# A fused adaLN block on one core: ring and order of the modulation rows, and the first three convolution blocks

## The chip, the core and the metric

The kernel runs on one core of a Trainium2 chip. The metric is the device time of one execution in microseconds; lower is better. A core has a matmul engine (TensorE, PE in the profile, with its weight loads as PEld), VectorE (DVE), ScalarE (ACT), GpSimd (POOL) and SyncE (SP, which here only issues transfers), and 16 DMA engines that carry every transfer. TensorE writes to PSUM, from which VectorE and ScalarE read.

## What is computed

The input u has shape (4, 1024, 2048). A small product makes six modulation vectors of 2048 for each of the four batch entries; then come a state-space convolution and a dense layer with a low-rank update, each behind a layer norm and a gate. Cut to what matters:

```python
mod = (silu(c) @ wmod).reshape(4, 6, 1, -1)        # wmod: 2048 x 12288
sa, ca, ga, sb, cb, gb = (mod[:, i] for i in range(6))
ga = sign(ga) * maximum(abs(ga), 0.25)             # gb likewise
h = layernorm(x) * (1 + ca) + sa
x = x + ga * (causal_conv(h, K) + D[0] * h)        # K: 2048 taps from the S4 parameters
h = layernorm(x) * (1 + cb) + sb
x = x + gb * (h @ W.T + bias + low_rank_update(h))
```

The convolution runs along the axis of 2048, with one kernel K for all rows. The 4096 rows of x make 32 blocks of 128.

## The kernel before, in words

**Modulation.** `wmod` is read in sections of 2048 columns: section 0 is the shift sa, 1 the scale ca, 2 the gate ga, and 4, 3, 5 belong to the second half. A section has 16 *rows*, tiles of 128 x 2048 f32 (1 MB). `mod_load` issues a row from SP (L312) into a tile `wm`; `mod_mm` (L317) takes it with four matmuls of 512 columns (eight records each time in the profile) into one PSUM tile `modps`. The generator `section(sec, pools)` does one row per step, alternates between the pools it is given, and ends with the section's last step: a column of scales for sa and ca, for the gate `mod_gate`, which leaves a tile of gate values `gas` (`mg` in the profile) and a copy in memory, `gad`. Two pools hold rows: `wmp` with WM = 3 tiles for the whole first part, and `wms` with WMS = 2 tiles, which lives until `st.close()`. Sections 1 and 0 use both, section 2 only `wmp`. `rows` is the generator that runs through section 0 and then section 2.

**Convolution.** For block r, `load(r)` reads x (L562) into one of four tiles, `stats(r)` makes mean and deviation on VectorE, and `conv_prep` (`prep(r)`) normalizes on VectorE (L557), transposes in four chunks on TensorE (L578), applies ca and sa on ScalarE (L582), and splits into half-precision high and low parts, `hc` and `hs`. `conv_mm` multiplies with the Toeplitz tiles of K (`kh`, `kl`, L614) in two halves (q = 0, 1) of three families each, and collects them in a tile y. Its argument `tick` is called between families and lets other work be issued there; `pace(n)` is called ahead of each group of matmuls with the columns that it streams.

**Early blocks.** The first blocks are begun before all modulation is there. Blocks 0 and 1 are prepared without the shift, which is convolved by itself (`shift_conv`, L397; broadcast from memory and added by `shift_add`, L414). The first EARLY = 3 blocks are convolved without the gate. When the gate is there, `gate_tile` broadcasts it over the partitions with four matmuls (`gps`, L674), VectorE scales it (L675), and `conv_late` applies gate and residual to each early y (L650, L651). `conv_post` stores y (`x1d`, L656), makes the sum of squares on ScalarE (L660, which overwrites the tile of x), and finishes the second norm's statistics; after it the x tile can take block r + 4. Later blocks apply gate and residual inside `conv_mm` (L633, L640, L641).

**Pacing.** During the early blocks `pace` takes one step of `rows` for each ROWC = 2400 columns and queues the group of convolution matmuls behind the last row's matmuls: `tc.issue_after(ins)` puts an instruction behind another on the same engine. Otherwise the order of an engine's queue is laid down at build time by a scheduler that follows the program's order and fills gaps.

**Fill.** Low-rank merging of W (`prep_lora`, `merge`) and the rows of sections 4, 3 and 5 form one generator `fill`, of which `step()` takes one step at the letters S of PLAN within each block. Blocks below R0 = 6 take a step only at every third call and only above EARLY.

The y tiles come from a pool of EARLY tiles, which all 32 blocks go through.

```python
for r in range(2):
    ys[r] = k.conv_mm(pl, hs.pop(r), xs[r], lambda: None, True, pace)
    load(r + 2)
stats(2)
take(prep(2), 9)
k.shift_conv(msm)
k.shift_add(pl["g"], [ys[r][0] for r in range(2)])
...
ys[2] = k.conv_mm(pl, hs.pop(2), xs[2], lambda: take(nxt, 1), True, pace)
take(nxt, 9)
take(rows, 40)
k.gat = k.gate_tile(pl["g"], 0)
```

Of the kernel before, what the change touches and what calls it, by code (L numbers as in the profile page):

```python
# [34 lines left out]
class Net:  # L35
# [557 lines left out]
                v.tensor_tensor(lo[:, sl], src, hi[:, sl], SUB)  # L593
            yield

    def conv_mm(self, pl, hs, x, tick, early, pace=lambda n: nullcontext()):
        nc, v = self.nc, self.nc.vector
        hc, hs = hs
        y = pl["y"].tile([P, D], F32, tag="y", name="y")
        yv = y.rearrange("p (j e t) -> p j e t", e=2, t=P)  # L600
        if not early:
            gv = self.gat.rearrange("p (j e t) -> p j e t", e=2, t=P)
        sums = pl["sm"].tile([P, 2], F32, tag="sums", name="sums")

        def family(ps, f, q, first):
            pf = ps.rearrange("p j t -> p (j t)")
            last = 4 * q + 3
            for i in range(last + 1):
                o = P * max(0, i - 4 * q)
                k0 = P * max(0, 4 * q - i)  # L610
                with pace(3 * (512 - o)):
                    for x, z in ((0, 0), (0, 1), (1, 0)):
                        h = hs[x][:, i] if f == 0 else hc[x][:, 2 * i + 2 - f]
                        nc.tensor.matmul(  # L614
                            pf[:, o:512], h, self.kf[f][z][:, ds(k0, 512 - o)],
                            start=first, stop=(i == last and (x, z) == (1, 0)), skip_group_check=True,
                        )
                        first = False
                if i == 3 and q == 1:
                    tick()  # L620

        for q in range(2):
            jj = slice(4 * q, 4 * q + 4)
            pa = self.acc.tile([P, 4, P], F32, tag="a", name="ya")
            family(pa, 0, q, True)
            qs = pl["t"].tile([P, 4, P], F32, tag="qs", name="qs")
            self.lasta = nc.scalar.copy(qs, pa)  # L627
            tick()
            pb = self.acc.tile([P, 4, P], F32, tag="a", name="yb")
            family(pb, 2, q, True)  # L630
            self.lastv = v.tensor_tensor(yv[:, jj, 1, :], pb, qs, ADD)
            if not early:
                v.tensor_tensor(yv[:, jj, 1, :], yv[:, jj, 1, :], gv[:, jj, 1, :], MUL)  # L633
            tick()
            family(pa, 1, q, False)
            sl = ds(1024 * q, 1024)
            if early:
                nc.scalar.copy(yv[:, jj, 0, :], pa)
            else:
                v.tensor_tensor(yv[:, jj, 0, :], pa, gv[:, jj, 0, :], MUL)  # L640
                v.scalar_tensor_tensor(y[:, sl], y[:, sl], 1.0, x[:, sl], MUL, ADD, accum_out=sums[:, q : q + 1])  # L641
            tick()
        return y, sums
# [21 lines left out]
    def gate_tile(self, pool, b):  # L665

        nc, v = self.nc, self.nc.vector
        t = pool.tile([P, D], F32, tag="gat", name="gat")
        s = self.hinv[:, b : b + 1]
        if b == 0:  # L670
            for q in range(4):
                ps = self.tps.tile([P, 512], F32, tag="t", name="gps")
                row = self.ident[:, 32 * q + b : 32 * q + b + 1].to_broadcast([P, P])
                nc.tensor.matmul(ps, row, self.gas, start=True, stop=True)  # L674
                v.tensor_scalar(t[:, ds(512 * q, 512)], ps, s, self.kinv, MUL, MUL)  # L675
        else:
            nc.sync.dma_start(out=t, in_=self.gad[b].partition_broadcast(P))
            v.tensor_scalar(t, t, s, self.kinv, MUL, MUL)
        return t
# [131 lines left out]
ACC, TPS = 5, 2  # L811
PLAN = ("PNSL", "NL", "NSL", "NTL", "SL", "SL", "SL", "SL", "FSL", "SSL")
LPLAN = ("LL", "LL", "LL", "LL", "L", "0", "")
R0 = 6
WM, WMS = 3, 2
ROWC = 2400
EARLY = 3
X0 = 11
LEFT0 = 30
KT = (0, 5, 6, 10)  # L820
# [11 lines left out]
def net(ctx: ExitStack, tc: tile.TileContext, io):  # L832
    nc = tc.nc
    k = Net(ctx, tc, io)
# [10 lines left out]
    pl = {}  # L845
    wmp = pool(right, "wm", WM, "right")
    msm = pool(right, "msm", 1, "right")
# [4 lines left out]
    def section(sec, pools):  # L852
        for q in range(16):
            if q == 0:
                k.mod_begin()
            k.mod_mm(k.mod_load(pools[q % len(pools)], sec, q), q)
            yield
        if sec == 0:
            k.sa = k.mod_column(msm, k.kpool, "sa", 0.0)
            k.hinv = k.fold_scale(msm, k.ca, k.sa, "fs1")  # L860
        elif sec == 1:
            k.ca = k.mod_column(msm, k.kpool, "ca", 1.0)
        elif sec == 2:
            k.gas, (k.gad,) = k.mod_gate(msm, "gad")
        elif sec == 4:
            k.cb = k.mod_column(msm, k.cst, "cb", 1.0)
        elif sec == 3:
            k.sb = k.mod_column(msm, k.cst, "sb", 0.0)
        else:
            _, k.gbd = k.mod_gate(msm, "gbd", io["bias"])  # L870
        yield
# [8 lines left out]
    def take(g, n):  # L880
        for _ in range(n):
            next(g, None)

    pl["sm"] = pool(left, "p1sm", 4)
    for name, bufs in (("h", 2), ("n", 1), ("t", 2), ("y", EARLY), ("g", 1)):
        pl[name] = pool(left, "p1" + name, bufs)
    st = ExitStack()
    toe = k.toeplitz(pool(st, "st", 1, "right"))
    wms = pool(st, "wms", WMS, "right")
# [3 lines left out]
    xs, hs, sts, ys = {}, {}, {}, {}  # L893

    def prep(r, shift=True):
        return k.conv_prep(pl, r, xs[r], sts.pop(r), hs, shift)

    def load(r):
        if r < 4:
            with tc.issue_after(k.lastw.ins):  # L900
                xs[r] = k.conv_load(pl, r)
        else:
            xs[r] = k.conv_load(pl, r)

    def stats(r):
        sts[r] = k.stats(pl, xs[r], "1")

    n = 0
# [6 lines left out]
        n += 1  # L915
    k.early_scale(msm)
    load(1)
    rows = (x for sec, w in ((0, (wms, wmp)), (2, (wmp,))) for x in section(sec, w))
    stats(0)
    take(prep(0, False), 9)  # L920
    with tc.issue_after(k.last.ins):
# [4 lines left out]
    cols = [0]  # L926

    def pace(n):

        cols[0] += n  # L930
        while cols[0] >= ROWC:
            cols[0] -= ROWC
            take(rows, 1)
        return tc.issue_after(k.last.ins)

    for r in range(2):
        ys[r] = k.conv_mm(pl, hs.pop(r), xs[r], lambda: None, True, pace)
        load(r + 2)
    stats(2)
    take(prep(2), 9)  # L940
    k.shift_conv(msm)
    k.shift_add(pl["g"], [ys[r][0] for r in range(2)])
    st.close()
    for name in ("lora", "mrg"):
# [46 lines left out]
    calls = [0]  # L991

    def step():
        if r < R0:

            calls[0] += 1
            if r > EARLY and calls[0] % 3 == 0:
                with tc.issue_after(k.lasta.ins), tc.issue_after(k.lastv.ins):
                    next(fill)
        elif "w" not in pr and next(fill, 0) == 0:  # L1000
            early()

    stats(3)
    nxt = prep(3)
    ys[2] = k.conv_mm(pl, hs.pop(2), xs[2], lambda: take(nxt, 1), True, pace)
    take(nxt, 9)
    take(rows, 40)
    k.gat = k.gate_tile(pl["g"], 0)
    ratio = k.kpool.tile([P, 1], F32, tag="rat", name="rat")
    nc.vector.tensor_tensor(ratio, k.einv, k.hs[:, 0:1], MUL)  # L1010
    for r in range(EARLY):
        k.conv_late(xs[r], *ys[r], ratio if r < 2 else 1.0)
        k.conv_post(pl, r, xs.pop(r), *ys[r])
        if r < 2:
            load(r + 4)
    stats(EARLY + 1)
    nxt = prep(EARLY + 1)
    take(nxt, 1)
    with tc.issue_after(k.lastw.ins):
        next(fill)  # L1020
    post = None
    for r in range(EARLY, 32):
        if EARLY + 2 < r + 2 < 32:
            load(r + 2)
        if r % 8 == 0:
            k.gat = k.gate_tile(pl["g"], r // 8)
        if r == 31:
            load_w(0, ORDER[1])
        if r == LEFT0:
            while "w" not in pr:  # L1030
                step()
            lgen = next_left(0)
        plan = iter(PLAN)
        follow = []

        def tick():
            for a in next(plan):
                if a == "S":
                    step()
                elif a == "P" and post:  # L1040
                    k.conv_post(pl, *post)
                elif a == "L" and r >= LEFT0:
                    take(lgen, 1)
                elif a == "N":
                    take(nxt, 1)
                elif a == "T" and r + 2 < 32:
                    stats(r + 2)
                elif a == "F" and r + 2 < 32:
                    follow.append(prep(r + 2))
                    take(follow[0], 1)  # L1050

        y = k.conv_mm(pl, hs.pop(r), xs[r], tick, False)
        tick()
        take(nxt, 9)
        post = (r, xs.pop(r), *y)
        nxt = follow[0] if follow else iter(())
# [96 lines left out]
```

## Time and profile before

| what | value |
|---|---|
| median of 3 runs | 2136.88 us (2131.98 to 2142.14) |
| the profiled execution | 2140.44 us, of which the span 2138.5 us |
| mean granted TensorE clock of that execution | 0.988 |
| ScalarE busy by the page | 925.3 us (43%) |
| transfers | 484.11 MB, mean 226 GB/s |
| first ten slices (53.5 us each), GB/s | 372 355 354 238 182 225 294 281 253 262 |

The page divides the span into 40 slices and gives each engine's busy share in tenths. A wait list names for each waiting instruction what released it. A timeline gives the start and length of each instruction or run of like instructions, and in brackets how long the engine stood idle before it and for what. Matmul records overlap, since matmuls are pipelined: the time of a 512-column matmul in a row of them is seen from one start to the next.

### The profile page before, as it was taken

How to read it: one execution, taken by the hardware profiler on the slowest of the kernel's cores; microseconds unless marked ns; L12 is line 12 of the kernel's file. 1: busy time of each engine (PE TensorE's matmuls, PEld its weight loads, DVE VectorE, ACT ScalarE, POOL GpSimd, SP SyncE). 2: the span in 40 equal slices, each digit the busy share in tenths (PEclk: the TensorE clock that was granted, in tenths of full speed). 3: DMA queues.
4: the chain of work that ended last, by engine and by line, in shares of the span. 5: the costliest groups of instructions: out<-in, count | busy, mean ns of one | idle time of the engine just before them, and what ended most of it. 6: DMA issues, size and time to landing. Idle time of an engine off the chain costs nothing.

```text
span 2138.5 us, 28420 instructions
## 1 busy us (share of the span) xinstructions
PE 2078.8 (97%) x11113; PEld 1024.8 (48%) x11113; DVE 1309.8 (61%) x2351; ACT 925.3 (43%) x1697; POOL 6.2 (0%) x18
## 2 busy tenths in 40 slices
PE   6888999999999999999999999999999999999998
PEld 2334554555555555654545545555444444444444
DVE  5538989989899999765565565575533333332323
ACT  1323876777677778745454555555200000000000
POOL 0000000000000000000000000000000000000000
PEclk7999999999999999999999999999999999999999
DMA  9896467766886456397564564564794545454542
GB/s 372 355 354 238 182 225 294 281 253 262 304 310 227 170 192 232 134 358 270 195 242 178 202 237 177 208 230 173 285 347 158 188 154 168 162 176 160 176 158 69
DMA packets 127236, 484.11 MB, mean 226 GB/s; under 512 B 13608, under 2 KB 13768, under 8 KB 95998
## 3 DMA queue, kind: packets, MB, share of 16 engines
q1 hardware_dynamic: 126192, 477.55, 61.3%
q10 hardware_dynamic: 526, 2.63, 0.4%
q8 instruction: 87, 1.43, 0.3%
q0 software_dynamic: 384, 2.11, 0.2%
q14 instruction: 47, 0.39, 0.0%
HBM read 326.94 MB, written 155.30 MB: 226 GB/s over the span
## 4 chain that ended last, share of the span: by engine, by line
PE 57%; issue 25%; DVE 3%; DMA 2%; ACT 1%; POOLq 0%; SPq 0%; POOL 0%; DVEq 0%
PE fZ L750 23%; PE fY L750 15%; PE fX L750 15%; PE tp L700 2%; PE ya L614 1%; DMA gb<-gbd 1%; PE yb L614 1%; DMA w<-wcd 0%; DVE y L641 0%; ACT x L660 0%; DMA x<-x1d 0%; DVE wch L514 0%; DVE lf L713 0%; DVE st L540 0%; DVE y L640 0%
## 5 line engine op out<-in xcount | busy, mean ns | idle before, releaser
L750 PEld LDWEIGHTS <-lf 128*128 128x128 f16 x5376 | 525.9, 98 | 620.6 <-issue 0.9
L750 PE MATMUL fZ<-w,lf 128*128 128x512 f16 x2304 | 514.1, 379 | 0.6 <-ACT p L758 0.6
L750 PE MATMUL fY<-w,lf 128*128 128x512 f16 x1536 | 342.1, 379 | 0.0
L750 PE MATMUL fX<-w,lf 128*128 128x512 f16 x1536 | 342.1, 379 | 0.0
L614 PEld LDWEIGHTS <-hc 128*128 128x128 f16 x2304 | 215.1, 98 | 197.0 <-issue 33.4
L768 DVE TENSOR_TENSOR xo<-xo,gb 128x512 f32<-128x512 f32 x128 | 87.6, 690 | 237.8 <-DMA xo<-x1d 226.5
L614 PE MATMUL ya<-kh,hs 128*128 128x512 f16 (+3 forms) x768 | 194.6, 328 | 3.0 <-DVE kh L284 2.6
L582 ACT ACTIVATE t<-tp,sa,ca 128x128 f32<-128x128 f32 x480 | 186.9, 467 | 15.5 <-PE tp L578 15.5
L614 PE MATMUL yb<-kh,hc 128*128 128x512 f16 (+3 forms) x768 | 192.2, 327 | 0.2 <-DVE y L640 0.2
L614 PE MATMUL ya<-kh,hc 128*128 128x512 f16 (+3 forms) x768 | 190.8, 326 | 0.9 <-ACT qs L627 0.8
L758 ACT COPY p<-fZ 128x512 f32<-128x512 f32 x64 | 37.2, 582 | 294.1 <-PE fZ L750 275.4
L614 PEld LDWEIGHTS <-hs 128*128 128x128 f16 x1152 | 107.1, 98 | 104.7 <-issue 27.8
L702 ACT ACTIVATE gt<-tp,sb,cb 128x256 f32<-128x256 f32 x256 | 124.7, 573 | 62.5 <-PE tp L700 61.0
L758 ACT COPY p<-fX 128x512 f32<-128x512 f32 x32 | 18.7, 585 | 305.1 <-PE fX L750 225.8
L317 PE MATMUL modps<-wm,sct 128*32 128x512 f32 x768 | 118.4, 666 | 24.2 <-DMA wm<-in_wmod 24.1
L614 PE MATMUL ya<-kl,hs 128*128 128x512 f16 (+3 forms) x384 | 125.9, 328 | 0.7 <-DVE kl L285 0.7
L614 PE MATMUL yb<-kl,hc 128*128 128x512 f16 (+3 forms) x384 | 125.6, 327 | 0.2 <-DVE kl L285 0.2
L614 PE MATMUL ya<-kl,hc 128*128 128x512 f16 (+3 forms) x384 | 125.1, 326 | 0.0
L773 DVE TENSOR_TENSOR fin<-fX,gb 128x512 f32<-128x512 f32 x32 | 22.1, 691 | 127.3 <-PE fX L750 127.2
L578 PE MATMUL tp<-ident,n 128*128 128x128 f32 x512 | 79.6, 282 | 14.9 <-ACT t L582 7.3
L593 DVE TENSOR_TENSOR hc<-t,hc 128x512 f16<-128x512 f32 x128 | 87.8, 686 | 7.5 <-ACT hc L592 7.2
L486 PE MATMUL lps<-lbh,lac 128*128 128x512 f16 x256 | 86.0, 379 | 2.3 <-DVE we L488 1.5
(265 smaller groups left out, 2223.4 us busy)
## 6 DMA issues: line engine op xcount, KB each, us to landing
wm<-in_wmod SPq DMA_DIRECT2D x96, 1024.0 KB
lfd<-lf SPq DMA_DIRECT2D x112, 512.0 KB
lf<-lfd SPq DMA_DIRECT2D x112, 512.0 KB
x<-in_x SPq DMA_DIRECT2D x32, 1024.0 KB
x1d<-y SPq DMA_DIRECT2D x32, 1024.0 KB
x<-x1d SPq DMA_DIRECT2D x32, 1024.0 KB
xo<-x1d SPq DMA_DIRECT2D x128, 256.0 KB
out<-xo SPq DMA_DIRECT2D x128, 256.0 KB
```

Of the source, the lines that this page charges most:

```text
L317: self.last = self.nc.tensor.matmul(self.modps[32 * g : 32 * g + 32, :], self.sct[:, j].rearrange("p r b -> p (r b)"), w[:, ds(512 * g, 512)],
L486: nc.tensor.matmul(ps, la[:, x, k, h], y[:, k, osl], start=(n == 0), stop=(n == 5))
L578: nc.tensor.transpose(tp[:, k], n[:, ds(P * (c0 + k), P)], self.ident)
L582: nc.scalar.activation(t[:, k], tp[:, k], AF.Identity, bias=self.sa[:, c, b : b + 1], scale=self.ca[:, c, b : b + 1],)
L593: v.tensor_tensor(lo[:, sl], src, hi[:, sl], SUB)
L614: nc.tensor.matmul(pf[:, o:512], h, self.kf[f][z][:, ds(k0, 512 - o)], start=first, stop=(i == last and (x, z) == (1, 0)), skip_group_chec ...
L700: nc.tensor.transpose(tp[:, c, r], xs[r][:, ds(P * (c0 + c), P)], self.ident)
L702: nc.scalar.activation(t[:, c0 + c], tp[:, c], AF.Identity, bias=self.sb[:, c0 + c, b : b + 1], scale=self.cb[:, c0 + c, b : b + 1],)
L750: nc.tensor.matmul(ps[name], lf[i][:, k, x, :], wc[i][k // 4][:, k % 4, y, :], start=(first and n == 0), stop=(n == 3 * HC - 1), skip_grou ...
L758: nc.scalar.copy(t, ps[name])
L768: v.tensor_tensor(x, x, self.gbias[:, h], ADD)
L773: v.tensor_tensor(t, cv, self.gbt[:, h], MUL)
```

## The change

- The pool `wms` gets three tiles (WMS = 3), and section 2 uses both pools as sections 0 and 1 do: a ring of six for all three.
- ROWC goes from 2400 to 2700; `rows` is taken to its end right after block 1 has been issued.
- EARLY goes from 3 to 2: only blocks 0 and 1 are convolved without the gate, and the pool of y has two tiles. Block 2 is convolved in the main loop with the gate inside `conv_mm`; the gate tile, the late updates of blocks 0 and 1, their `conv_post` and the loads of x for blocks 4 and 5 are issued ahead of it.
- The shift's convolution, the statistics and the preparation of block 2 become a generator, `third`, that the ticks of block 1 advance.
- In block 2 each group of matmuls after the first GCOL = 11000 columns is queued behind the last matmul of the gate's broadcast (`behind`, `self.gps`).
- R0 goes from 6 to 5, and below it the fill takes a step at every second call instead of every third; with EARLY = 2 these are blocks 3 and 4.

```diff
-                nc.tensor.matmul(ps, row, self.gas, start=True, stop=True)
+                self.gps = nc.tensor.matmul(ps, row, self.gas, start=True, stop=True)
...
-R0 = 6
-WM, WMS = 3, 2
-ROWC = 2400
-EARLY = 3
+R0 = 5
+WM, WMS = 3, 3
+ROWC = 2700
+GCOL = 11000
+EARLY = 2
...
-    rows = (x for sec, w in ((0, (wms, wmp)), (2, (wmp,))) for x in section(sec, w))
+    rows = (x for sec in (0, 2) for x in section(sec, (wms, wmp)))
...
-    for r in range(2):
-        ys[r] = k.conv_mm(pl, hs.pop(r), xs[r], lambda: None, True, pace)
-        load(r + 2)
-    stats(2)
-    take(prep(2), 9)
-    k.shift_conv(msm)
+    def third():
+        while not hasattr(k, "hinv"):
+            yield
+        k.shift_conv(msm)
+        stats(2)
+        yield from prep(2)
+
+    ys[0] = k.conv_mm(pl, hs.pop(0), xs[0], lambda: None, True, pace)
+    load(2)
+    nxt = third()
+    ys[1] = k.conv_mm(pl, hs.pop(1), xs[1], lambda: take(nxt, 1), True, pace)
+    load(3)
+    take(rows, 40)
+    take(nxt, 40)
     k.shift_add(pl["g"], [ys[r][0] for r in range(2)])
...
-            if r > EARLY and calls[0] % 3 == 0:
+            if r > EARLY and calls[0] % 2 == 0:
...
-    stats(3)
-    nxt = prep(3)
-    ys[2] = k.conv_mm(pl, hs.pop(2), xs[2], lambda: take(nxt, 1), True, pace)
-    take(nxt, 9)
-    take(rows, 40)
     k.gat = k.gate_tile(pl["g"], 0)
...
     for r in range(EARLY):
-        k.conv_late(xs[r], *ys[r], ratio if r < 2 else 1.0)
+        k.conv_late(xs[r], *ys[r], ratio)
         k.conv_post(pl, r, xs.pop(r), *ys[r])
-        if r < 2:
-            load(r + 4)
-    stats(EARLY + 1)
-    nxt = prep(EARLY + 1)
+        load(r + 4)
+    stats(3)
+    nxt = prep(3)
...
+    def behind(n):
+        cols[0] += n
+        return tc.issue_after(k.gps.ins) if cols[0] > GCOL else nullcontext()
...
-        if EARLY + 2 < r + 2 < 32:
+        if EARLY + 4 <= r + 2 < 32:
             load(r + 2)
...
-        y = k.conv_mm(pl, hs.pop(r), xs[r], tick, False)
+        y = k.conv_mm(pl, hs.pop(r), xs[r], tick, False, behind if r == EARLY else none)
```

More of the change, by code (lines that the diff above doesn't have):

```diff
@@ L594, in conv_prep, with conv_mm @@
             yield
-    def conv_mm(self, pl, hs, x, tick, early, pace=lambda n: nullcontext()):
+    def conv_mm(self, pl, hs, x, tick, early, pace):
         nc, v = self.nc, self.nc.vector
@@ L896, in prep, with none @@
         return k.conv_prep(pl, r, xs[r], sts.pop(r), hs, shift)
+    def none(n):
+        return nullcontext()
     def load(r):
@@ L1020, in net @@
         next(fill)
+    cols[0] = 0
+    def behind(n):
+        cols[0] += n
+        return tc.issue_after(k.gps.ins) if cols[0] > GCOL else nullcontext()
     post = None
     for r in range(EARLY, 32):
-        if EARLY + 2 < r + 2 < 32:
+        if EARLY + 4 <= r + 2 < 32:
             load(r + 2)
```

## The prediction

> **What bounds the kernel now.** I read the page first: the shares by engine and the 40 slices.
>
> ```profile
> span 2138.5 us, 28420 instructions
> PE 2078.8 (97%) x11113; PEld 1024.8 (48%) x11113; DVE 1309.8 (61%) x2351; ACT 925.3 (43%) x1697; POOL 6.2 (0%) x18
> PE   6888999999999999999999999999999999999998
> DVE  5538989989899999765565565575533333332323
> ```
>
> TensorE is busy all but 59.7 us, and the change adds and removes no matmul. So it can win only idle time or half-clock time of TensorE. The slices put the loss at the front. Summing the idle gaps of TensorE's timeline by stretch: 24.8 us before 72 us, 9.4 from there to 162.4 (blocks 0 and 1), 7.3 to 222, 12.0 to 925 (blocks 4 to 31), 0.6 after. The waits of TensorE in the first 500 us name the causes:
>
> ```profile
> PE modps L317 <- DMA wm<-in_wmod: 24.1, 14, 9.1
> PE tp L578 <- DVE n L557: 6.3, 2, 6.1
> PE kbps L263 <- DMA kb<-kd: 4.1, 1, 4.1
> ```
>
> The columns are total us, times, longest. Next TensorE's timeline (start, length, then the idle time before it in brackets):
>
> ```profile
> 104.84 1.06 PE L317 MATMUL modps<-wm,sct 128*32 128x512 f32 x8 [0.42 <-DMA wm<-in_wmod]
> 114.81 1.07 PE L317 MATMUL modps<-wm,sct 128*32 128x512 f32 x8 [1.77 <-DMA wm<-in_wmod]
> 117.97 1.06 PE L317 MATMUL modps<-wm,sct 128*32 128x512 f32 x8 [1.00 <-DMA wm<-in_wmod]
> 145.82 1.69 PE L317 MATMUL modps<-wm,sct 128*32 128x512 f32 x8 [2.98 <-DMA wm<-in_wmod]
> 154.61 1.07 PE L317 MATMUL modps<-wm,sct 128*32 128x512 f32 x8 [0.75 <-DMA wm<-in_wmod]
> 157.19 1.06 PE L317 MATMUL modps<-wm,sct 128*32 128x512 f32 x8 [0.91 <-DMA wm<-in_wmod]
> 182.16 1.94 PE L674 MATMUL gps<-mg,ident 128*128 128x512 f32 x4
> 212.28 1.97 PE L578 MATMUL tp<-ident,n 128*128 128x128 f32 x8 [6.11 <-DVE n L557]
> ```
>
> Place A: rows of section 2 keep blocks 0 and 1 waiting for 0.42+1.77+1.00+2.98+0.75+0.91 = 7.8 us. Place B: the transposes of block 4 wait 6.1 us, and gaps of 0.7 and 0.4 us follow. To see whether A is bandwidth or buffers I took 5 us windows. Columns: length, busy us of PE, PEld, DVE, ACT, POOL, then the granted clock, the DMA share and GB/s:
>
> ```profile
> 125.00:130.00 5.00, 4.63 (x38) 3.14 (x37) 2.48 (x5) 3.89 (x11) 0.00 (x0) 1.00 0.75 306
> 130.00:135.00 5.00, 4.73 (x30) 2.52 (x30) 1.72 (x5) 1.57 (x4) 0.53 (x1) 0.75 0.63 215
> 140.00:145.00 5.00, 2.85 (x21) 0.98 (x19) 0.00 (x0) 0.58 (x1) 0.00 (x0) 1.00 1.00 410
> 210.00:215.00 5.00, 1.97 (x9) 1.58 (x9) 5.00 (x11) 1.56 (x5) 0.00 (x0) 0.60 1.01 419
> ```
>
> The DMA engines were a third idle at 130 us and TensorE starved at 143: rows could not be sent for want of a free tile. The wait list of SP's queue agrees ("L312 <- PE modps": 62.0 us, 24 times, between 40 and 230 us). At B, VectorE is full (5.00 of 5), and x of block 4 was late, by SP's timeline:
>
> ```profile
> 192.45 0.35 SPq L656 DMA_DIRECT2D x1d<-y  x1
> 195.82 0.35 SPq L562 DMA_DIRECT2D x<-in_x  x1
> ```
>
> **What the Trainium skill says.** "TensorE: Matmul & The Clock Gate", Part 1: the array falls to half clock after an idle window of about 3.4 us and needs about 3.4 us of activity to return. The trace agrees: clock 0.60 above, and a 512-column matmul takes 0.63 us at 217 us against 0.38 at 223. "DMA: Bandwidth & Descriptors", Bandwidth: large reads reach 425 GB/s; here 410 to 427 in full windows, so a row of 1.05 MB takes about 2.45 us. "Perfetto Trace Analysis", Identifying Performance Opportunities: repeated bubbles on the engine that should be full can mean too few buffers; that is place A. "TensorE", Architectural detail: ScalarE and VectorE queues are strict FIFO, so what stands ahead of block 4's normalization delays it; VectorE's timeline shows 1.2 us updates (L650, L651) back to back from 185 to 202.
>
> **The change, part by part.**
>
> *Ring of six, 2700 columns a row.* Before, section 0 alternates two and three tiles, so row q+4 waits for row q; section 2 has three. A block has 3 x 13824 = 41472 columns; 512 take 0.217 us, so 17.6 us. At 2700 columns a row, TensorE spends 1.14 us on convolution and 1.0 on the row: 2.14 us, against 2.45 us of DMA. The ring starts 15 us of rows ahead. Block 0 with its 14 rows, transposes of block 1 (2.2) and the sa column (0.7) costs 17.6+14+2.9 = 34.5 us. Block 1 with 15 rows, transposes of block 2 (2.4) and the shift's matmuls (4.1) costs 39.1. In these 73.6 us the DMA engines must bring about 26 rows not yet there at 72 us, x2 and the shift's broadcast: 28 x 2.45 = 69. So TensorE bounds it, narrowly. The 7.8 us go, and so does the half clock from 146.1 to 149.5 after the longest gap (half of 3.4 = 1.7). The half clock from 132.5 to 135.9 follows the small shift matmuls, and I leave it. At most 9.5 us; because the balance is narrow and the last row now queues behind x3 (2.45 us, with six tiles ahead of it), I take 8, with 4 and 9.5 as ends. Before 72 us nothing falls: the start of block 0 hangs on kb and kh (4.1 and 2.6 us waits), not on tiles; 0 to 1.
>
> *Third block with its gate, broadcast near its front.* The gate is ready at 161.1 (mg, last step at L347) but TensorE takes the broadcast at 182.2, behind block 2. Now it goes behind the last row by about 4 us (157.2 to 161.1 before), during which TensorE has the first half q=0 of block 2: 11520 columns, 4.9 us. GCOL 11000 keeps the second half behind it, so at worst the gate costs 1 us there. The broadcast itself (3.8 us) only moves. VectorE loses one late update (2 x (1.2+1.3) = 5.0) and gains the gate products and residual in block 2 (two of 0.69 at L633, two of 0.63-0.69 at L640 for ScalarE's 0.58 copy, two of 1.23 at L641 = 5.2): zero. What moves is time: the update of block 0 ended 11.3 us after the broadcast began (182.16 to 193.45), its Square at 195.7, and x4 left at 195.8. Counted from the end of block 1, x4 left at +33.4 (195.8-162.4) and should leave at about +19. TensorE needs block 4 at 2 x 17.6 + 3.8 + 2.4 + 2.4 = +44, and x4 lands at about +25, so its DMA is off the path. What is late next is VectorE: gate 3.3, updates 10.2, small steps 1.6, y of block 2 6.8, preparation of block 3 6.2 and of block 4 (statistics 3.4, normalization 1.35, half of 6.2) 7.9, y of block 3's first half 3.4: 39.4 us after +6.5, so +46. Block 3's statistics fit before +6.5, where VectorE is idle. So of 7.3 us idle and the 3.9 of half clock after it (8.9 us from 212.3, less 1.1 idle, halved) about 2 us come back: 9 gained, ends 3 and 11.
>
> *y on two tiles.* Block 2's y takes y0's tile, free when its store and Square are done, about +18. Its PSUM tiles hold meanwhile: four of five are block 2's, so TensorE runs to about +26. Cost 0; without that cover, the delay of the store beyond +26. In the loop a store leaves when y is done and the tile is next written over a block later: 0.
>
> *Third block's preparation as a generator, pace to none after block 1.* The same instructions; the schedule already ran block 2's transposes within block 1 (119.6 to 126). 0.
>
> *Fill from block 3, every second call; loads of x from r=4.* The loads are the same. The fill's first steps are mostly ScalarE: squares and copies of la and lb, 4.5+4.1+5.5+7.9 = 22 us (L432, L445, L449, L459, L460), at 235 to 283 us before. Now up to a block earlier, where preparation and VectorE's backlog are tight. ScalarE has about 6 us free in a block of 20. Cost 0 to 4, taken 1. SP gets the fill's loads earlier too: the slow rival. From block 5 on the fill runs one block ahead, and it was done long before block 30.
>
> Sum: 8 + 9 - 1 = 16 us. The profiled execution took 2140.44 us (span 2138.5, 1.9 around it), which is 3.6 above the median of 2136.88. The gain is a difference, so I take it from the median: 2136.9 - 16 = 2121.
>
> **Rivals.** (1) *VectorE takes over the wait.* The chain gate, two updates, preparations is FIFO and full; the +46 above could be +52 if block 3's statistics are queued behind the updates (3.4 + 1.35). Then blocks 3 and 4 wait some 6 us, at half clock for 3 more: 16 - 8 = 8 gained, 2129. For it: 5.00 of 5 at 210. Against: VectorE idles from 134 to 145, when x3 could come. (2) *Rows stay bound by transfers.* If the rows get 2.8 us each (375 GB/s, as in the slower windows), 28 take 78 us: A gives 3 instead of 8, the gate shifts as much: 11 - 3 = 8, 2129 too. For it: full windows at 100 to 120. (3) *Slower: SP's queue.* It is in order, and the fill's tile loads wait there for their tile: one at L470 held SP from 291.4 to 315.2, 23.9 us, at no cost since nothing behind it was due. If one stands ahead of the store of y0 or the load of x4 near 165 us, y0's tile comes free 24 us late, at +42 against +26: 16 us of stall on full PSUM, the next block's x as late again (about 8), 4 of half clock; 28 lost against 16 won: 2149. It decides from 26 us of lateness on. Against: at 176.7 SP already waited for the store with nothing stuck ahead.
>
> **How the numbers follow.** Forecast 2121: 0.63. Rival 1: 0.17, rival 2: 0.10, rival 3: 0.10. About 0.5% (10.7 us) is what a measurement of this kernel can tell from no change. The ends of the terms give gains from 4+3-4 = 3 to 20.5: 2134 to 2116; repeats spread by 10 us, so 2111 to 2134, which takes in rivals 1 and 2. Faster: nearly all of the forecast (0.60) and a fifth of rivals 1 and 2 (0.06), 0.66. Slower: 0.09 of rival 3. Same: 0.25.
>
> **What would show it.** Right: waits of L317 for wm near zero after 75 us; DMA share near 1 from 75 to 135; block 1 ending near 154; gps at 158 to 161; x4 leaving near 173; no idle above 2 us before block 4, clock 1.00 there; TensorE idle about 47 us. Wrong: a gap of 5 us or more before tp of block 3 or 4, the last row later than 155, or an SP wait over 15 us ahead of x1d.

## The result, and the profile after

| | kernel before | changed kernel |
|---|---|---|
| median of 20 runs | 2141.88 us | 2141.03 us |
| ratio of the runs, 95% interval | | 0.9999 (0.9987 to 1.001) |
| span of the profiled execution | 2138.5 us | 2140.1 us |

No change that can be measured, where 16 us had been forecast. The forecast of 2121 us was counted from 2136.88 us, the median of the first three runs of the kernel before; the median of twenty lies 5.0 us higher. The gain is therefore judged by the ratio and not by the absolute time. The page of the changed kernel, its first part and TensorE's slices:

```profile
span 2140.1 us, 28438 instructions
PE 2082.4 (97%) x11113; PEld 1026.1 (48%) x11113; DVE 1308.4 (61%) x2353; ACT 923.7 (43%) x1695; POOL 6.3 (0%) x18
PE   7898999999999999999999999999999999999998
```

The third slice (107 to 160 us) is fuller than before and the fourth (160 to 214) no fuller. The waits of TensorE in the first 500 us (us in total, times, longest) show a swap. `modps` is the tile that collects the rows, `gps` the gate's broadcast, `tp` the transposes that prepare a block, `ya` and `yb` (further below) the convolution:

```profile
PE modps L317 <- DMA wm<-in_wmod: 14.1, 9, 7.9
PE gps L674 <- DVE mg L347: 9.9, 1, 9.9
...
PE tp L578 <- DVE n L557: 0.8, 1, 0.8
```

The waits for rows fell from 24.1 to 14.1 us. Of what remains, 13.4 us lie ahead of block 0 and 0.7 us are at 236.6 us, at a row of a later section; the 7.8 us of place A are gone. The waits of transposes for a normalization fell from 6.3 to 0.8 us. In their place stands a wait of 9.9 us that the kernel before did not have: the gate's broadcast waits for the gate's values (`mg`). TensorE's timeline around it:

```profile
158.32 1.07 PE L317 MATMUL modps<-wm,sct 128*32 128x512 f32 x8
169.31 5.81 PE L674 MATMUL gps<-mg,ident 128*128 128x512 f32 x8 [9.93 <-DVE mg L347]
```

The last row ends at 159.4 and nothing follows for 9.9 us. The broadcast then takes 5.8 us instead of the 3.8 of before, since the array has gone to half clock: the trace has it from 163.3 to 173.5 us, and the last column but two is 0.50 here:

```profile
165.00:170.00 5.00, 0.69 (x1) 0.50 (x2) 3.49 (x6) 0.63 (x1) 0.00 (x0) 0.50 1.01 422
```

What VectorE did meanwhile, from its own timeline:

```profile
159.05 2.29 DVE L414 TENSOR_TENSOR y<-y,gsb 128x2048 f32<-128x2048 f32 x1 [7.87 <-ACT y L638]
161.26 2.46 DVE L540 BATCH_NORM_STATS2 st<-x 128x6 f32<-128x512 f32 x4
...
165.13 1.35 DVE L557 TENSOR_SCALAR n<-x,mv,rs 128x2048 f32<-128x2048 f32 x1
166.39 0.68 DVE L342 COPY mg<-modps 128x512 f32<-128x512 f32 x1
...
168.57 0.69 DVE L347 SCALAR_TENSOR_TENSOR mg<-mg,mg 128x512 f32<-128x512 f32 x1
```

The gate's sums were ready at 159.4. VectorE's queue held the shift's addition to block 1, and the statistics and normalization of block 3, ahead of the copy: 7.0 us from 159.4 to 166.4. The chain itself took the other 2.9.

And the row had been there. SP's timeline has its transfer leaving at 143.74, behind it only small ones until 157.37:

```profile
143.74 0.33 SPq L312 DMA_DIRECT2D wm<-in_wmod  x1
144.12 1.44 SPq L424 DMA_DIRECT2D lws<-in_coeffs  x2
145.60 1.24 SPq L424 DMA_DIRECT2D lws<-in_scales  x2
157.37 0.40 SPq L426 DMA_DIRECT2D la<-in_A  x1
```

By the windows of 5 us (granted clock, DMA share and GB/s at the end of each line), the traffic was over soon after 150. The first and the last of these lines are used further below:

```profile
115.00:120.00 5.00, 4.73 (x22) 2.85 (x22) 0.45 (x2) 0.00 (x0) 0.54 (x1) 0.50 0.49 203
150.00:155.00 5.00, 5.00 (x36) 1.61 (x33) 0.69 (x1) 0.00 (x0) 0.00 (x0) 1.00 0.32 102
155.00:160.00 5.00, 4.39 (x31) 1.46 (x29) 0.95 (x1) 0.58 (x1) 0.00 (x0) 1.00 0.22 77
160.00:165.00 5.00, 0.00 (x0) 0.00 (x0) 4.59 (x10) 0.20 (x1) 0.00 (x0) 0.83 1.03 357
225.00:230.00 5.00, 5.00 (x41) 2.62 (x40) 3.95 (x10) 5.00 (x11) 0.00 (x0) 1.00 0.25 43
```

Nothing at all moved from 154 to 157 us. So the row lay in its tile for some 5 to 7 us while TensorE did convolution: the pace of one step in 2700 columns had kept it back.

How far is TensorE at 160 us? Both kernels have all 384 row matmuls behind them there, the changed one also 45 more of the convolution's. At an average of 0.163 us (17.6 us by 108 a block) that is 7.3 us of lead. Of it 3.2 us come from the earlier start of the convolution in this execution (next paragraph), which leaves some 4 for the change. 30 of the 45 belong to block 2: most of its first half of 36 had run between the rows of block 1. At 170 us the count is 15 behind that of the kernel before.

**The sum.** The first convolution matmul starts at 71.7 us in the profile of before and at 68.5 in that of after; over all profiles shown here it starts between 65.3 and 71.7, whatever the edit, so this start says nothing about the change. The table therefore runs from there to the first matmul of the dense layer, in us. "Half" is half of the time that TensorE worked at half clock, added up from the trace; the rest is work.

| | length | idle | half | rest |
|---|---|---|---|---|
| before | 846.9 | 28.8 | 7.3 | 810.8 |
| after | 850.4 | 29.4 | 8.8 | 812.2 |

Idle time by stretch, before and after, each gap counted where it ends: from the first convolution matmul to 162 us 9.4 and 2.9; to 222 us 7.3 and 11.1; from there to 925 us 12.0 and 15.3.

Put in order by cause, with the half clock that goes with each wait, 18.2 us of the kernel before are gone: 6.5 of idle time up to 162 us, 6.1 of it from 170 to 222 us (9.9 of the 11.1 above are the gate's), and 5.6 of half clock, 1.7 behind the longest wait for a row and 3.9 at block 4. And 19.4 us are new: 12.0 at the gate (9.9 idle, 2.1 half clock), 3.3 of half clock at the shift's matmuls (5.0 against 1.7, see E8), and 4.1 between 222 and 260 us (2.4 idle, 1.7 half clock, see E3). The other 2.3 of the 3.5 us by which the lengths in the table differ are idle time after 260 us (0.9) and work. These are sums over one execution of each kernel.

### The profile page after: what moved, and what is told of

The parts are those of the page before. It is cut to its first block, busy times and chain, and to the rows that moved or that the text cites. A ratio compares the mean times of both kernels' runs of the same rounds, so it can differ in the third digit from the quotient of the medians.

```text
span 2140.1 us, 28438 instructions
## 1 busy us (share of the span) xinstructions
PE 2082.4 (97%) x11113; PEld 1026.1 (48%) x11113; DVE 1308.4 (61%) x2353; ACT 923.7 (43%) x1695; POOL 6.3 (0%) x18
## 4 chain that ended last, share of the span: by engine, by line
PE 67%; DVE 18%; ACT 6%; DMA 5%; issue 2%; SPq 0%; ACTq 0%; POOL 0%; DVEq 0%; POOLq 0%
PE fZ L750 22%; PE fY L750 15%; PE fX L750 15%; PE ya L614 5%; PE yb L614 3%; PE tp L700 3%; DVE wch L514 2%; PE modps L317 2%; DVE st L540 2%; DVE hc L593 2%; DVE y L641 2%; ACT x L660 2%; DMA wcd<-wch 1%; ACT t L582 1%; PE lps L486 1%
## 5 line engine op out<-in xcount | busy, mean ns | idle before, releaser
L582 ACT ACTIVATE t<-tp,sa,ca 128x128 f32<-128x128 f32 x480 | 188.1, 471 | 21.6 <-PE tp L578 12.9
L317 PE MATMUL modps<-wm,sct 128*32 128x512 f32 x768 | 118.8, 662 | 14.1 <-DMA wm<-in_wmod 14.1
```

Of the source, the lines that this page charges most:

```text
L317: self.last = self.nc.tensor.matmul(self.modps[32 * g : 32 * g + 32, :], self.sct[:, j].rearrange("p r b -> p (r b)"), w[:, ds(512 * g, 512)],
L582: nc.scalar.activation(t[:, k], tp[:, k], AF.Identity, bias=self.sa[:, c, b : b + 1], scale=self.ca[:, c, b : b + 1],)
```

## The experiments

All ratios are to the kernel before, with their 95% intervals; the changed kernel stands at 0.9999 (0.9987 to 1.001). "Below the changed kernel" is the difference of two ratios times 2142 us, and is uncertain by some 3 to 5 us; where the intervals overlap, the text says so. A line number in a profile of an edited kernel is up to four higher than in the kernel before where the edit adds lines.

**E1, the gate ahead of everything on VectorE.** `last` is the instruction at L347.

```diff
-        for y in ys:
-            self.nc.vector.tensor_tensor(y, y, g, ADD)
+        self.nc.vector.tensor_tensor(ys[0], ys[0], g, ADD)
+        with self.tc.issue_after(last.ins):
+            self.nc.vector.tensor_tensor(ys[1], ys[1], g, ADD)
...
-    stats(3)
-    nxt = prep(3)
-    take(nxt, 1)
+    with tc.issue_after(k.gate_op.ins):
+        stats(3)
+        nxt = prep(3)
+        take(nxt, 1)
```

> The changed kernel, with the shift's addition to y of block 1, and the statistics and normalization of block 3, queued on VectorE behind the last step of the gate's values (L347 of the changed kernel). Theory A (the win of the rows and of block 4 is there and is spent at the gate, because VectorE has 7.0 us of other work queued ahead of the gate's copy while TensorE has the broadcast next in its queue): the 9.9 us wait of gps falls to about 3, half clock after it goes or halves, and the time is 7 to 10 us below the changed kernel's, 0.995 to 0.997 of the kernel before. Rival B (VectorE and ScalarE bound blocks 3 to 24, so that time won before block 4 is given back there): the wait falls the same, and the time stays within 2 us of the kernel before. Rival C (the fill's earlier ScalarE steps take the win in blocks 4 and 5): the wait falls, block 4 starts 7 us earlier, and idle time of TensorE between 225 and 260 us grows above 6 us.

Measured: 1.0034 (1.0024 to 1.0044), about 7 us slower. The waits of TensorE between 160 and 265 us:

```profile
PE tp L579 <- ACT t L583: 3.1, 2, 1.9
PE gps L675 <- DVE mg L347: 3.0, 1, 3.0
PE modps L317 <- DMA wm<-in_wmod: 2.4, 1, 2.4
PE tp L579 <- DVE n L558: 1.8, 1, 1.8
PE ya L615 <- ACT hs L593: 1.3, 2, 0.9
```

The gate's wait fell to the chain's own 3.0 us, as all theories had it. But block 3's preparation, now behind the late updates, made new waits at 186 to 190 us and others at 231 and 251, and half clock followed at 190, 231 and 252 us: its loss went from 8.8 to 13.1 us. Theory A's time was wrong: here the work that was moved from ahead of the gate to behind it was waited for there.

**E2, nothing held behind the broadcast** (`GCOL = 1000000`).

> The changed kernel with GCOL = 1000000: nothing of block 2 is held behind the gate's broadcast. Theory A: the wait of gps vanishes, since TensorE has the second half of block 2 to do, but the broadcast comes some 12 us later on TensorE's queue than the gate's values, the late updates and the load of x for block 4 slide as in the kernel before, and half or more of the win is lost again by a wait of block 3 or 4; net 0 to 6 us below the kernel before. Rival B: within 2 us of the kernel before whatever the waits do.

Measured: 0.9995 (0.9986 to 1.0003). The wait of gps went; the broadcast moved to near the end of block 2, and waits for preparation and rows came at 183 and 208 to 211 us. Idle time from the first convolution matmul on fell from 29.4 to 24.6, and the loss at half clock rose from 8.8 to 10.1. The time alone doesn't tell A from B.

**E3, the fill paced as before.**

```diff
-R0 = 5
+R0 = 6
...
-            if r > EARLY and calls[0] % 2 == 0:
+            if r > 3 and calls[0] % 3 == 0:
```

> The changed kernel with the fill paced as before (R0 = 6, every third call in blocks 4 and 5). Theory A: idle time at the gate stays at 9.9 us, time within 2 us of the changed kernel. Rival C (the fill's earlier steps cost what was won): waits between 222 and 260 us fall from 2.5 to under 0.5 us, half clock at 238 goes, and the time falls by 4 us or more.

Measured: 0.9988 (0.9978 to 0.9999), 2.4 us below the changed kernel, with intervals that overlap. Between 222 and 260 us idle time fell from 2.5 to 0.1 us and the half clock at 238 went. The gate's wait stayed at 9.9. So the earlier fill does make waits: ScalarE has no free time in the changed kernel from 215 to 235 us (5.00 of 5 in the window from 225, shown above). What they cost is not clear of noise in this run alone; E7 against E2, the same edit without the hold, shows 6.4 us. Rival C is right in kind, with about half of the size that it claimed in this run.

**E4, the ring alone in the kernel before:** section 2 takes rows from both pools, two and three tiles.

```diff
-    rows = (x for sec, w in ((0, (wms, wmp)), (2, (wmp,))) for x in section(sec, w))
+    rows = (x for sec in (0, 2) for x in section(sec, (wms, wmp)))
```

> The kernel before with one edit: section 2 takes its rows from both pools (ring of 2 and 3 tiles), nothing else. The order of TensorE's queue is the same. Theory A: waits of L317 for rows between 100 and 160 us fall from 7.8 us to under 3, block 1 ends 5 to 8 us earlier, and since block 4's wait hangs on the chain behind block 2 (gps, updates, x4), all of it moves up with it: 5 to 9 us below the kernel before. Rival B: within 2 us of it. Rival D (rows bound by bandwidth, not tiles): waits stay above 6 us.

Measured: 0.9986 (0.9971 to 1.0002), not told apart from the kernel before. This ring has five tiles, not the six of the change. Row waits after 72 us fell only from 7.8 to 5.2, and the 7.1 us wait of block 4 stayed. At 260 us it led by 32 convolution matmuls (5.2 us, of which 2.2 is the earlier start); at 500 us by 4. Here some of the lead was given back in blocks 7 to 13, where waits grew by 3.3 us between 300 and 500.

**E5, statistics of block 3, then gate, then addition.** As E1, but the statistics and normalization of block 3 are issued ahead of the last rows, for the time in which VectorE stands idle (their three lines further down go):

```diff
     load(3)
-    take(rows, 40)
     take(nxt, 40)
+    stats(3)
+    nxt = prep(3)
+    take(nxt, 1)
+    take(rows, 40)
```

> The changed kernel with VectorE's queue ordered at block 2's front: statistics and normalization of block 3 first (x of block 3 lands near 148 us and VectorE stands idle from 133 to 159), then the gate's values, then the shift's addition to y of block 1. Theory A (the win is spent at the gate through VectorE's order): the wait of gps falls from 9.9 to about 3 us and, unlike with the gate put ahead of everything, block 3's transposes do not wait near 186 us; time 6 to 9 us below the changed kernel. Theory A' (the gate wait goes, but blocks 3 to 5 are bound by VectorE and ScalarE with the fill, so most comes back as waits between 180 and 260 us): 0 to 3 us below the changed kernel, idle time from 180 to 260 us above 6 us.

Measured: 0.9974 (0.9963 to 0.9986), 5.4 us below the changed kernel by the ratios. The wait of gps fell to 4.6 and not to 3: ScalarE's square root of the deviation stood behind the copy of block 1's last sum until 155.2, and VectorE waited 5.1 us for it. TensorE's line, then VectorE's:

```profile
160.29 6.23 PE L675 MATMUL gps<-mg,ident 128*128 128x512 f32 x8 [4.60 <-DVE mg L347]
```

```profile
155.45 0.16 DVE L71 RECIPROCAL rs<-r_t 128x1 f32<-128x1 f32 x1 [5.11 <-ACT r_t L70]
157.37 0.68 DVE L342 COPY mg<-modps 128x512 f32<-128x512 f32 x1
```

No wait came at 186. With E1 this shows that the order on VectorE costs the changed kernel some 5 us, which can be had back if the work ahead of the gate is put into VectorE's idle time, and not by putting it behind the gate.

**E6, the same with the fill as before.**

> The same order on VectorE, and the fill paced as before. Theory A': without the fill's ScalarE work in blocks 3 and 4 the waits from 180 to 260 us fall under 3 us, and the gate's win stays: 6 to 10 us below the kernel before. Rival B (time won before block 5 is always given back by block 24): within 3 us of the changed kernel with the fill as before (0.9988).

Measured: 0.996 (0.9947 to 0.9974). Idle time from 222 to 260 us fell from the 3.2 of E5 to 0.3. Rival B, that nothing won before block 5 can last, does not hold.

**E7, no hold, fill as before.**

> The changed kernel without the hold on block 2's second half (GCOL = 1000000) and with the fill paced as before. If the two costs are separate they add up: idle time from block 0 to the dense layer of 24.6 - 3.0 = 21 to 22 us and 4 to 6 us below the kernel before. Rival B: 0.999 as with either edit alone.

Measured: 0.9965 (0.9951 to 0.9978), faster than either edit alone: 7.3 us below the changed kernel, where E2 and E3 are 0.9 and 2.4 below it. Whether it is more than their sum the noise leaves open. Its profiled execution, at a span of 2138.8 us, is slower than its median of 2132.99 and has waits at 268 and 328 us, so the idle time expected of it cannot be checked in it.

**E8, the shift's matmuls in four groups.**

```diff
+            with self.tc.issue_after(self.lastc.ins):
                 nc.tensor.matmul(
                     ps[:, m:NC], self.kb[:, ds(P * m, P)], sa[:, 0 : NC - m],
...
+            if m % every == every - 1 and m < NC - 1:
+                yield
```

`lastc` is the last convolution matmul issued, `every` is 4; `third` prepares the statistics and normalization of block 2 first, then takes the groups one tick apart.

> The changed kernel with the shift's 16 small matmuls issued in four groups of four, each behind the convolution matmuls of another family of block 1, instead of in one stretch. If the one stretch of small matmuls (6.1 us at 111) is what sends TensorE to half clock from 112.1 to 122.3, that stretch goes, and 2 to 4 us with it in block 1; the time at the end falls by 2 to 4 us (no change if the gate's wait just grows by it, since the broadcast waits for the last row and the last row for the DMA).

Measured: 0.9976 (0.9966 to 0.9986), 4.9 us below the changed kernel. The shift in TensorE's timeline, first in the changed kernel, then spread:

```profile
111.06 6.06 PE L397 MATMUL gsp<-sae,kb 128*128 128x16 f32 x32 [1.13 <-DVE sae L394]
```

```profile
114.57 1.06 PE L398 MATMUL gsp<-sae,kb 128*128 128x16 f32 x8 [1.13 <-DVE sae L394]
...
119.30 1.01 PE L398 MATMUL gsp<-sae,kb 128*128 128x12 f32 x8
...
122.89 1.01 PE L398 MATMUL gsp<-sae,kb 128*128 128x8 f32 x8
```

In one stretch they take 6.1 us and half clock lasts from 112.1 to 122.3; in groups no half clock is recorded between 76 and 161 us. The kernel before had them in two stretches of 1.7 and 2.1 us with 3.4 us of half clock after. How long the spell is differs between executions: in the nine profiles with one stretch (the changed kernel, E1 to E3, E5 to E7, E11, E13) it is 3.4, 6.8 or 10.2 us long, so the changed kernel's profile shows the longest kind.

**E9, the three edits at once** (order of E5, fill of E3, spread of E8).

> The changed kernel with three edits at once: VectorE's order at block 2's front (statistics of block 3, gate, addition), the fill paced as before, the shift's matmuls in four groups. If the three costs are separate (5.4, 2.4 and 4.9 us below the changed kernel, each measured alone or in steps), they add up: 12 to 13 us below the changed kernel, ratio 0.994 to 0.995 to the kernel before. Rival B (a fixed bound of VectorE and ScalarE on blocks 3 to 24): no better than 0.996, the best of the earlier runs.

Measured: 0.9949 (0.9932 to 0.9967). The costs add up within the noise: 10.7 us below the changed kernel, of the 12.7 of the single steps.

**E10, the three edits without the hold.**

> The three edits and GCOL = 1000000. The remaining wait for the gate (4.6 us and half clock after it) goes, since block 2 runs on; the broadcast comes about 100 matmuls later, so block 3 and 4 get their x later. If the hold is what costs: 0.992 to 0.994. If an early gate pays for the hold: equal to or above the run with the hold.

Measured: 0.9958 (0.9944 to 0.9972), not told apart from E9. The wait of gps went; waits of 2.3 and 1.0 us for the preparation of block 3, and of 1.8 us at 264 for a copy on ScalarE, came. So the hold behind the broadcast has no clear worth and no clear cost here, where the gate waits 4.6 us. Where it waits 9.9 us the hold does cost: E7 is E3 without it, and stands 4.9 us lower, with intervals that just touch.

**E11, the ring undone in the changed kernel** (the `rows` line of before, WMS = 2, the pace at 2700).

> The changed kernel with the ring undone: section 2 on three tiles, section 0 on two and three, the pace at 2700. Theory A (the ring's tiles take 6 us of row waits away): waits of L317 for rows from 75 to 160 us come back to 5 us or more, block 1 ends 4 to 7 us later, time 3 to 7 us above the changed kernel. If the slower pace alone did it: no more than 2 us above.

Measured: 1.0013 (1.0000 to 1.0027), 3 us above the changed kernel, with intervals that overlap. TensorE's waits between 66 and 265 us:

```profile
PE gps L674 <- DVE mg L347: 7.1, 1, 7.1
PE modps L317 <- DMA wm<-in_wmod: 6.6, 7, 2.8
```

The row waits are back, 6.2 us of them up to 163 us. Part of what they cost is hidden in the gate's wait, which is 2.8 us shorter. So the trace shows that the sixth tile and the common ring take the waits away; a gain in time is not shown by this run.

**E12, the three edits with a row in 2500 columns.**

> The three edits and ROWC = 2500, so that the last row is taken within block 1 and not behind it. If the gate is late because the pace holds the last row back (the DMA engines are a third busy from 150 to 160 us in the changed kernel), the wait of gps falls from 4.6 to under 1 us and its half clock goes, 3 to 6 us below the same kernel at 2700. If rows are bound by transfers, waits of L317 for rows rise by as much and the time is the same.

Measured: 0.9911 (0.9892 to 0.993), 2123.67 us against 2142.13: the lowest median of the study, and clearly below both the kernel before and the changed one. Rows make no wait. The wait of gps is 4.0 us, not under 1, but it is another one. Two of the four broadcast matmuls run at once, and the others wait for a PSUM tile that VectorE (L679, `gat`) has not yet read:

```profile
PE gps L678 <- DVE gat L679: 4.0, 1, 4.0
```

**E13, the pace alone:** the changed kernel with `ROWC = 2500`.

> The changed kernel with ROWC = 2500 and nothing else; at this pace the last row stands within block 1, and the queue laid down at build time has the gate's copy ahead of block 3's statistics. If the pace is the cause of the late gate: the wait of gps falls from 9.9 to 4 us or less, time 6 to 9 us below the changed kernel (0.996 to 0.997). If VectorE's order by itself is the cause and the pace a detail: the same fall, and e15 equals e12. If rows are bound by transfers: waits of L317 for rows take its place and the time is that of the changed kernel.

Measured: 0.9955 (0.9939 to 0.9971), 9.4 us below the changed kernel, by one number. TensorE's timeline, then VectorE's:

```profile
151.41 1.06 PE L317 MATMUL modps<-wm,sct 128*32 128x512 f32 x8
155.47 1.98 PE L674 MATMUL gps<-mg,ident 128*128 128x512 f32 x4
161.46 3.78 PE L674 MATMUL gps<-mg,ident 128*128 128x512 f32 x4 [4.00 <-DVE gat L675]
```

```profile
152.54 0.69 DVE L342 COPY mg<-modps 128x512 f32<-128x512 f32 x1 [2.82 <-PE modps L317]
...
155.33 2.46 DVE L540 BATCH_NORM_STATS2 st<-x 128x6 f32<-128x512 f32 x4
```

The last row is taken at 151.4 instead of 158.3, VectorE is idle and waiting for it, and the queue laid down at build time now has the gate's copy ahead of block 3's statistics. The pace moves both the row and the order. It also moves what stands around the shift, whose one stretch ran at full clock in this profile, with no wait ahead and a spell of 3.4 us behind it instead of 10.2:

```profile
108.29 3.68 PE L397 MATMUL gsp<-sae,kb 128*128 128x16 f32 x32
```

So the 9.4 us may hold a part that belongs to the shift and not to the gate.

**E14, the three edits at 2400.**

> The three edits with ROWC = 2400, the pace of the kernel before. If the ring of six keeps rows ahead at this pace too: within 2 us of the run at 2500 (0.9911). If 2.02 us a row on TensorE against 2.45 us of DMA binds: waits of L317 for rows of 2 us or more with half clock after one, 2 to 4 us above it.

Measured: 0.9929 (0.9909 to 0.9949), 2125.0 us; its interval overlaps that of E12. No wait for rows from 66 to 265 us: the ring of six keeps rows ahead at the pace of the kernel before too, so the slower pace was not needed for it.

**E15, fill and spread at 2500, without the edit to VectorE's order.**

> The changed kernel with the fill as before, the shift's matmuls spread and ROWC = 2500, without the edit to VectorE's order. If the pace alone brings the gate in time: within 2 us of e12 (0.9911). If the explicit order is still worth something: 3 us or more above it.

Measured: 0.9939 (0.9918 to 0.9961), 2127.02 us, 12.9 us below the changed kernel. The middle lies 6 us above E12, but the intervals overlap, so whether the explicit order is still worth something at this pace stays open.

## Why the prediction was wrong, point by point

**The step that failed** is this: the gate's broadcast "goes behind the last row by about 4 us", "during which TensorE has the first half q=0 of block 2", so that "at worst the gate costs 1 us there". In the changed kernel's profile it cost 12.0 us: 9.9 of idle time, and 2.1 at half clock in the broadcast. Three things were missed in it.
- The cover was spent. The first half of block 2 had been drawn into block 1, where it filled the gaps between rows; 30 of its 36 matmuls had run when the last row came, and `behind` holds back the rest. I counted that work once as filling the waits for rows and again as cover. (Even unspent the cover would have been 30 matmuls, 10368 columns or 4.4 us, and not the 11520 columns of the prediction: GCOL = 11000 holds the last two groups of the first half.)
- The last row came late by choice and not by transfer. 82944 columns of two blocks at 2700 a step give 30 steps for 32, so the last row stands behind block 1, as the change intended, although its data were there. I looked for its price in the DMA queue (x3 ahead of it) and not in the pace. E13 shows this one number to be worth 9.4 us, row, order and a part at the shift together.
- VectorE's queue was taken to have block 3's statistics done before the gate. They stood in front of it, behind an addition that waited for the end of block 1: 7.0 us. The prediction named such an order only as rival 1, with its wait at blocks 3 and 4; it appeared at the gate. E5 shows 5.4 us for the order.

**The rows** (8 us taken). Right in mechanism: no row of sections 0 and 2 is waited for after block 0 begins, and the waits return in E11. The slower pace was not needed for it: E14 has no such wait at 2400. The sum for the two blocks was too small and did not agree with its own sign: 73.6 us from 72 us would end block 1 at 145.6 and not "near 154". The changed kernel's profile has 89.9 us from the first convolution matmul to the end of block 1 at 158.4; 4.4 of them are the 30 matmuls of block 2, 2.9 idle time and 5.0 half clock, which leaves 77.6 us of work. The term left out was the shift: `third` puts its 32 short matmuls into one stretch, and the half clock that I had left as it was (3.4 us long) became 10.2 us long in the profiled execution; E8 puts the one stretch at 4.9 us. The part by part text cost `third` at nothing.

**Block 4's x and its wait** (9 taken). By the trace it was right: the wait and its half clock are gone, 10 us together (6.1 and 3.9), although x of block 4 left at +25.7 from the end of block 1 and not at +19, the gate being late.

**The fill** (1 taken, 0 to 4). 2.4 us by E3, inside the range and not told apart from 1; 6.4 us without the hold (E7 against E2).

**y on two tiles, the loads** (0). Right as far as the trace shows: the store of block 0 left as soon as its y was ready, and VectorE waited 0.6 us in all for an x.

**Rivals.** Rival 2 is excluded by E12 and E14, where rows make no wait even at 2500 and 2400 columns. Rival 3 did not happen: L470 held SP for 7.9 us until 173.9 us, and the store of block 0 left at 181.75 us. Rival 1 is the nearest to what happened: VectorE's order took a part of the win, but at another place.

**The range.** The spread of repeats was allowed for at its lower end only (2116 to 2111). With the other end widened in the same way it would have reached 2139 us. The base of three runs, 5.0 us under the median of twenty, is in all of these absolute times.

Put together from the changed kernel up, the single costs must not be added: the pace (E13: 9.4), the shift in one stretch (E8: 4.9) and the fill (E3: 2.4) make 16.7 us, near the 16 that were forecast and not found, but E15, which undoes these three at once, stands 12.9 us below the changed kernel. With VectorE's order as well (E12) it is 18.8 us. E13 may hold a part of E8's (its profile differs at the shift too), and each difference is uncertain by some 3 to 5 us. What is shown is that undoing the costs leaves a kernel 0.9911 (0.9892 to 0.993) of the one before. That the two removed waits are what it gains by is read from the traces; no run undoes the third block's new place, and the two that test rings (E4, E11) differ from their partners by no more than the noise.

## What to carry to other kernels

Work that is pulled forward to fill one wait is no longer there to cover the next; count each stretch of cover once, and ask at every new wait what is left in the queue behind it. When a pace is slowed to match a transfer, check what hangs on its last step: here the data lay ready, and the consumer's own pace made the chain behind it late. Where the total is zero, undo the change's parts one by one: by the traces this zero was made of 18.2 us gone and 19.4 us new, and a version with the costs reduced (E12) beats both kernels.

## What the runs showed of the hardware that was not expected

A stretch of short matmuls was followed by half clock, as idle time is elsewhere in these traces. The 32 records of 16 columns and fewer followed an idle gap of only 1.1 us, TensorE counts as busy in them (4.73 of 5 us from 115 to 120), and the granted clock was 0.50 in that window. All nine profiles with the one stretch have such a spell, also E13 with no gap ahead of it; the six with groups of about 1.0 us between other matmuls (E8, E9, E10, E12, E14, E15) have none, three of them with the same gap of 1.1 us ahead. So the gap alone is not the cause. Two stretches of about 2 us were followed by half clock in the kernel before and by none in E4. "TensorE: Matmul & The Clock Gate", Part 1 in the Trainium skill, ties the clock to how busy the array has been recently; the busy share of the profile did not tell that here.

Waits shorter than the idle window of about 3.4 us with which the prediction reckons were followed by half clock too: 2.98 us at 145.8 in the kernel before, 1.9 and 2.4 us at 231 and 251 in E1. Of two waits of 1.8 us one was (at 264 in E10) and one was not (at 114.8 in the kernel before). The spells from block 0 to the dense layer are 3.4, 6.8 or 10.2 us long in all profiles.
